# A four-stage decoder on one core: score scale folded into the queries, half tiles, and rotary partners fetched by DMA and combined on GpSimd

## The chip, the cores and the metric

The kernel runs on one core of one Trainium2 chip, in fp32. The time is that of the device, in microseconds (us). The engines are named as the profile names them: PE is TensorE, DVE is VectorE, ACT is ScalarE, POOL is GpSimd, and SP is SyncE, which issues the transfers (DMAs). Each engine works through its own queue in order and waits on semaphores for the others.

## The reference, cut to what matters

The input is 64 sequences of 128 positions and 256 features. Six sublayers are added to it in turn, each on a layer-normalized input. The change lies in the second, fourth and fifth of them, and touches names in the others.

```python
# 1 state-space layer (mamba)
# 2 cross attention, 16 heads of 16, with rotary positions
q = q * cos + rotate_half(q) * sin        # rotate_half: (x1, x2) -> (-x2, x1)
k = k * cos + rotate_half(k) * sin        # x1, x2: the two halves of a head's 16 features
attn_w = softmax(q @ k.T * 16 ** -0.5); out = attn_w @ v @ Wo.T + bo
# 3 gated recurrence: c = sig(f) * c + sig(i) * tanh(g), per step of 128; h = tanh(x Wo + c Uo)
# 4 self attention: 16 query heads, 4 key/value heads, q and k scaled by a factor per position
# 5 cross attention with one head of 256
# 6 mixture of 8 experts, 2 per token, and one shared expert
```

In this kernel the third sublayer steps over the 64 sequences, one step a sequence.

## The kernel before, in words

Sequences are taken in groups of G = 4, so a group has T = 512 columns and there are 16 groups. Activations `X[g]` stay in SBUF for the whole run. There are four stages, each with its own SBUF and PSUM pools. Stage 1 is the state-space layer (0 to 785 us of the profiled execution). Stage 2 is the rotary cross attention together with the recurrence (785 to about 2000). Stage 3 is self attention, the wide cross attention and the routing (about 2000 to 3070). Stage 4 is the experts (3070 to 3482).

In stages 2 and 3 the work is written as Python generators. `run(tasks)` gives each task a turn at which it starts and then advances all active ones by turns, one `yield` at a time. In stage 2 `cross_inputs(g)` starts at turn 16g, the eight `cross_attention(g, b, c)` of a group (four sequences b, two halves c of the heads) at 16g + 16 + 4b + 2c, and `recurrence(g)` at 16g + 42. In stage 3 `self_inputs(g)`, `self_attention(g, b, c)` and `cross_and_route(g)` are placed in the same way. This sets the order in which instructions are handed in; the framework's scheduler then places them, and fixes the order on every engine when the program is built. One group's inputs are thus prepared while the attention of the group before and the recurrence of the one before that are under way.

The parts that matter here:

- `norm` (L166) computes the statistics on DVE, then takes the power −0.5 on POOL (`power`, L163, tile ln_rstd), then writes xn on DVE with four operations, one a sequence (L189). `transposed` (L194) makes pt_ln on PE and copies its two halves to xnT on ACT (L202) and DVE (L204).
- `cross_inputs` (L490): for q and for k two projections into PSUM (proj), of 128 features each, are copied with their bias to raw on ACT (L506). PE multiplies raw by a constant 128x128 permutation with signs (rot, L512). DVE multiplies rot by the sine (L514), POOL multiplies raw by the cosine (L518) and adds both into qT or kT (L519).
- `heads` (L224) is one half-set of eight heads of one sequence. POOL builds a block-diagonal key tile kbd (L284), PE forms the scores s in PSUM (L236), and DVE takes their maximum per row and head (L241) and multiplies it by minus the score scale (L242, tile mx). ACT takes eight exponentials with that bias into e (L245). PE transposes them to pt (L250), ACT and DVE each copy one half to eT (L252, L253), and PE forms av from eT and v (L261).
- v (L532 and stage 3) carries 16 values and 16 ones per head; POOL sets the ones each time with a memset (L533).
- `recurrence` (L565): the input part xg (L572 to L583), then per sequence pu on PE (L593), the sum and tanh in xg, and kept, new and c2 on DVE (L604, L605, L609). Its output xo is stored to DRAM and added to `X[g]` by `self_inputs` in stage 3 (POOL L643, ACT L644, POOL L645).

The PSUM of stages 2 and 3 is divided as `{"mm": 3, "s": 1, "pt": 1, "av": 1}`[...].

Of the kernel before, what the change touches and what calls it, by code (L numbers as in the profile page):

```python
# [15 lines left out]
P = 128  # L16
# [7 lines left out]
C_IDENT, C_UPPER, C_LOWER, C_ROT, C_COS, C_SIN, C_RF, C_ONES = (P * i for i in range(8))  # L24
C_HEAD = 8 * P
# [37 lines left out]
def tile_decoder(ctx: ExitStack, tc: tile.TileContext, a: dict, out: bass.AP):  # L63
# [35 lines left out]
    rot = cst[:, C_ROT:C_ROT + P]  # L99
# [57 lines left out]
    nc.gpsimd.tensor_scalar_mul(fu, fu, 0.5)  # L157

# [35 lines left out]
    def transposed(work, ps, xn, bufs=2):  # L194

        xnT = work.tile([P, 2, T], F32, tag="xnT", name="xnT", bufs=bufs)
        for c in range(2):
            pt = ps.tile([P, T], F32, tag="mm", name="pt_ln")
            for b in range(G):
                nc.tensor.transpose(pt[:, b * P:(b + 1) * P], xn[:, b, c * P:(c + 1) * P], ident)  # L200
            if c == 0:
                nc.scalar.copy(xnT[:, c, :], pt)  # L202
            else:
                nc.vector.tensor_copy(xnT[:, c, :], pt)  # L204
        return xnT

    def project(ps, w, m0, m, rhs):

        o = ps.tile([P, T], F32, tag="mm", name="proj")
        for k in range(2):  # L210
            nc.tensor.matmul(  # L211
                o[:m, :], lhsT=w[:, k, m0:m0 + m], rhs=rhs[:, k, :], start=(k == 0), stop=(k == 1)
            )
        return o

    def project_rows(dst, lhsT, w, b, m=None):

        for k in range(2):
            nc.tensor.matmul(  # L219
                dst, lhsT=lhsT[:, k, b * P:(b + 1) * P], rhs=w[:, k, :] if m is None else w[:, k, m],  # L220
                start=(k == 0), stop=(k == 1),
            )

    def heads(work, ps, b, c, state, q, kbd, v, scale):  # L224
# [9 lines left out]
        for hf in range(2):  # L234
# [4 lines left out]
            )  # L239
        mx = work.tile([P, 8], F32, tag="mx", name="mx", bufs=2)  # L240
        nc.vector.tensor_reduce(mx, s, AX.X, ALU.max)  # L241
        nc.vector.tensor_scalar(mx, mx, -scale, None, ALU.mult)  # L242
        e = work.tile([P, 8, P], F32, tag="e", name="e", bufs=2)
        for h in range(8):
            nc.scalar.activation(e[:, h, :], s[:, h, :], AF.Exp, bias=mx[:, h:h + 1], scale=scale)  # L245
        yield
        yield
        pt = ps.tile([P, 8, P], F32, tag="pt", name="pt")
        for h in range(8):
            nc.tensor.transpose(pt[:, h, :], e[:, h, :], ident)  # L250
        eT = work.tile([P, 8, P], F32, tag="eT", name="eT", bufs=2)
        nc.scalar.copy(eT[:, 0:4, :], pt[:, 0:4, :])  # L252
        nc.vector.tensor_copy(eT[:, 4:8, :], pt[:, 4:8, :])  # L253
# [6 lines left out]
        for vals, which, j, place in vh(c):  # L260
            nc.tensor.matmul(  # L261
                av[j * 32:j * 32 + 32, place, :], lhsT=vals, rhs=eT[:, which, :],
                start=True, stop=True,
            )
        if c == 1:
# [14 lines left out]
            state[b] = o  # L280

# [197 lines left out]
    for c in range(2):  # L479
        for w in (lwq, lwk, lwv):  # L480
            nc.gpsimd.tensor_scalar_mul(w[:, c, :], w[:, c, :], lg[:, c:c + 1])

# [7 lines left out]
    def cross_inputs(g, work, ps, got):  # L490
# [9 lines left out]
        for w, bias, src, tag in ((xwq, xbq, xnT, "qT"), (xwk, xbk, cT, "kT")):  # L500
            t = work.tile([P, 2, T], F32, tag=tag, name=tag, bufs=2)
            raws = []
            for c in range(2):
                pp = project(ps, w, c * P, P, src)
                raw = work.tile([P, T], F32, tag="raw", name="raw", bufs=2)
                nc.scalar.activation(raw, pp, AF.Identity, bias=bias[:, c:c + 1])  # L506
                raws.append(raw)
            yield
            yield
            for c, raw in enumerate(raws):  # L510
                pr = ps.tile([P, T], F32, tag="mm", name="rot")
                nc.tensor.matmul(pr, lhsT=rot, rhs=raw, start=True, stop=True)  # L512
                tv = t[:, c, :].rearrange("p (b t) -> p b t", b=G)
                nc.vector.tensor_tensor(  # L514
                    tv, pr.rearrange("p (b t) -> p b t", b=G), mid(sinT, G), ALU.mult
                )
                rv = raw.rearrange("p (b t) -> p b t", b=G)
                nc.gpsimd.tensor_tensor(out=rv, in0=rv, in1=mid(cosT, G), op=ALU.mult)  # L518
                nc.gpsimd.tensor_tensor(out=tv, in0=tv, in1=rv, op=ALU.add)  # L519
            got[g, tag] = t  # L520
            yield
            yield
        got[g, "c"] = cT

    def cross_attention(g, b, c, work, ps, got):
        tb = slice(b * P, (b + 1) * P)

        def values():
            if c == 0:
                pv = ps.tile([P, T], F32, tag="mm", name="pv")  # L530
                project_rows(pv[:, :D], got[g, "c"], xwv, b)
                v = work.tile([P, 16, 32], F32, tag="v", name="v", bufs=3)  # L532
                nc.gpsimd.memset(v[:, :, 16:32], 1.0)  # L533
# [7 lines left out]
                (v[:, h, :], h % 8, h % 4, h // 4) for h in range(8 * c, 8 * c + 8)  # L541
# [3 lines left out]
            work, ps, b, c, got, got[g, "qT"][:, c, tb],  # L545
            lambda: block_diagonal(work, got[g, "kT"][:, c, tb]), values, 0.25,
# [18 lines left out]
    def recurrence(g, work, ps, got):  # L565
# [6 lines left out]
        xg = work.tile([P, 6, T], F32, tag="xg", name="xg")  # L572
        xo = work.tile([P, G, D], F32, tag="xo", name="xo")
        for part in range(2):
            for c in range(part * 3, part * 3 + 3):
                pp = project(ps, fx, c * P, P, xnT)
                nc.scalar.activation(xg[:, c, :], pp, AF.Identity, bias=fb[:, c:c + 1])
# [7 lines left out]
        for b in range(G):  # L585
            tb = slice(b * P, (b + 1) * P)
            c2 = got["c2"]
            for c0, n in ((0, 4), (4, 2)):
# [8 lines left out]
                pre = xg[:, c0:c0 + n, tb]  # L597
# [6 lines left out]
            nc.vector.scalar_tensor_tensor(kept, xg[:, 0:2, tb], 1.0, c2, ALU.add, ALU.mult)  # L604
            nc.vector.scalar_tensor_tensor(  # L605
                new, xg[:, 2:4, tb], 1.0, xg[:, 4:6, tb], ALU.add, ALU.mult
            )
# [7 lines left out]
    with phase_pool("work2", "left") as work, phase_pool("ps2", space=PSUM) as psp:  # L615
        ps = PsumPool(psp, {"mm": 3, "s": 1, "pt": 1, "av": 1})
        got = {"c2": c2}
# [21 lines left out]
    def self_inputs(g, work, ps, hc, got):  # L639
# [28 lines left out]
        v = work.tile([P, G * 4, 32], F32, tag="v", name="v", bufs=2)  # L668
        nc.gpsimd.memset(v[:, :, 16:32], 1.0)
# [3 lines left out]
    def self_attention(g, b, c, work, ps, got):  # L673
# [3 lines left out]
        def keys():  # L677
            if c == 0:
# [6 lines left out]
                (v[:, b * 4 + j, :], slice(j, 8, 4), j, slice(2 * c, 2 * c + 2)) for j in range(4)  # L685
            ], 1.0 / 16,
# [16 lines left out]
    def wide_attention(g, work, ps):  # L703
        cT = load_ctx(work, g, 1)
# [21 lines left out]
        for b in range(G):  # L726
            tb = slice(b * P, (b + 1) * P)
            for k in range(2):
                nc.tensor.matmul(
                    s[:, b, :], lhsT=qT[:, k, tb], rhs=cT[:, k, tb], start=(k == 0), stop=(k == 1)  # L730
                )
        mx = work.tile([P, G], F32, tag="mx2", name="mx2", bufs=2)
        nc.vector.tensor_reduce(mx, s, AX.X, ALU.max)

        nc.vector.tensor_tensor(mx, mx, qb, ALU.add)
        nc.vector.tensor_tensor(mx, qb, mx, ALU.subtract)
        nc.vector.tensor_scalar(mx, mx, 1.0 / 16, None, ALU.mult)
        e = work.tile([P, G, P], F32, tag="e2", name="e2")
        den = work.tile([P, G], F32, tag="den2", name="den2", bufs=2)
        for b in range(G):  # L740
            nc.scalar.activation(
                e[:, b, :], s[:, b, :], AF.Exp, bias=mx[:, b:b + 1], scale=1.0 / 16,
# [32 lines left out]
    def route(g, work, ps, got):  # L775
# [6 lines left out]
        nc.sync.dma_start(out=XN[g], in_=xnT)  # L782
# [68 lines left out]
    with phase_pool("work3", "left") as work, phase_pool("ps3", space=PSUM) as psp:  # L851
        ps = PsumPool(psp, {"mm": 3, "s": 1, "pt": 1, "av": 1})
# [19 lines left out]
        nc.scalar.copy(yu, pb[:, :D + 1])  # L872
        nc.scalar.copy(ymb, pb[:, D + 1:D + 3])
        for c in range(2):
# [6 lines left out]
            nc.scalar.copy(ym[:, c, :], pw[:, :D])  # L881
# [7 lines left out]
        got = {"full": base}  # L889
# [11 lines left out]
    with phase_pool("work4", "left") as work, phase_pool("ps4", space=PSUM) as psp:  # L901
# [161 lines left out]
        def shared_expert(g):  # L1063
# [5 lines left out]
                gated(project(ps, msg, c * P, P, xnT), project(ps, msu, c * P, P, xnT), f"hs{c}")  # L1069
# [36 lines left out]
def constants():  # L1106
# [10 lines left out]
    for m in range(P):  # L1117
        if d[m] < 8:
            c[m + 8, C_ROT + m] = -1.0
        else:  # L1120
            c[m - 8, C_ROT + m] = 1.0
    inv = (f(1.0) / np.power(f(10000.0), np.arange(0, 16, 2, dtype=f) / f(16))).astype(f)
    ang = i.astype(f)[None, :] * inv[d % 8][:, None]
    c[:, C_COS:C_COS + P] = np.cos(ang.astype(np.float64))
    c[:, C_SIN:C_SIN + P] = np.sin(ang.astype(np.float64))
# [25 lines left out]
def laid_out(v):  # L1151
# [6 lines left out]
    def cat(names, suffix=""):  # L1158
        return np.concatenate([v[f"L0_ffn_{n}"].T for n in names], axis=1)

    b, s, d = v["ctx_1024"].shape
# [8 lines left out]
        "xwq": t("L0_xattn_Wq"), "xbq": v["L0_xattn_bq"], "xwk": t("L0_xattn_Wk"), "xbk": v["L0_xattn_bk"],  # L1170
# [37 lines left out]
```

## Time and profile before

| | us |
|---|---|
| median of 3 runs | 3532.04 (3531.86 to 3532.44) |
| the profiled execution | 3483.77 |
| its span | 3482.0 |
| PE / DVE / ACT / POOL busy | 3176.3 / 2273.2 / 1471.3 / 1302.8 |
| mean granted PE clock | 0.948 |

The span is the time from the first to the last instruction in the trace; the execution has 1.8 us around it. The profiled execution is one run, and was 48 us shorter than the median. Busy times of different engines overlap. Times of places in the trace are counted from the span's start. A half-set of attention occurs 128 times in stage 2 and 128 times in stage 3.

### The profile page before, as it was taken

The numbers are of one execution on the slowest core, as the hardware profiler recorded it, in microseconds if no ns is written. First come the engines' busy times: TensorE is split into PE (matmuls) and PEld (weight loads), VectorE is DVE, ScalarE is ACT, GpSimd is POOL, SyncE is SP. The second block draws the span as 40 slices with busy tenths as digits, with TensorE's granted clock in tenths as the row PEclk, the third lists the DMA queues.
The fourth block names the chain that finished last, engine by engine and source line by source line (L and its number), as shares of the span: only waits on it lengthen the run. The fifth ranks groups of instructions, "written<-read, shape, count | busy, mean of one in ns | idle before, by whom it ended". The sixth has DMA issues, their size and how long they took to land.

```text
span 3482.0 us, 48744 instructions
## 1 busy us (share of the span) xinstructions
PE 3176.3 (91%) x17486; PEld 2033.9 (58%) x17486; DVE 2273.2 (65%) x5498; ACT 1471.3 (42%) x3781; POOL 1302.8 (37%) x1290
## 2 busy tenths in 40 slices
PE   7899999998999999999999767999999999779989
PEld 4555555554666666666666633556566655468845
DVE  7999889965565556655565344777777777543355
ACT  3333333334545555455545234555555555213301
POOL 2444444455332323332332064233333333223276
PEclk9999999999999999999999878999998999789999
DMA  9980000001000000000000011101010101157655
GB/s 312 343 283 1 1 1 1 1 14 30 13 19 13 19 13 13 14 18 19 13 13 7 34 50 41 37 32 42 32 43 32 42 31 43 60 167 227 200 182 180
DMA packets 170658, 229.48 MB, mean 66 GB/s; under 512 B 19504, under 2 KB 142896, under 8 KB 170416
## 3 DMA queue, kind: packets, MB, share of 16 engines
q1 hardware_dynamic: 152448, 180.19, 16.0%
q0 software_dynamic: 17968, 46.18, 4.3%
q8 instruction: 138, 2.26, 0.3%
q14 instruction: 104, 0.85, 0.1%
HBM read 113.71 MB, written 127.93 MB: 69 GB/s over the span
## 4 chain that ended last, share of the span: by engine, by line
PE 62%; DVE 24%; POOL 6%; ACT 4%; DMA 2%; issue 2%; ACTq 0%; DVEq 0%; POOLq 0%; SPq 0%
PE proj L211 17%; PE pt L250 7%; PE s L236 6%; PE pu L593 5%; DVE acc L333 4%; DVE xn L189 4%; PE pgu L1019 4%; PE pv L219 3%; PE pt_ln L200 2%; PE av L261 2%; DVE mx L241 2%; PE pd L1028 2%; PE pxo L219 2%; PE pd L1079 1%; PE po L439 1%
## 5 line engine op out<-in xcount | busy, mean ns | idle before, releaser
L245 ACT ACTIVATE e<-s,mx 128x128 f32<-128x128 f32 x2048 | 555.9, 383 | 479.6 <-DVE mx L242 390.0
L284 POOL TENSOR_TENSOR kbd<-kT,consts 128x512 f32<-128x512 f32 x192 | 202.9, 1057 | 682.3 <-PE s L236 674.0
L253 DVE COPY eT<-pt 128x512 f32<-128x512 f32 x256 | 176.0, 687 | 392.7 <-ACT eT L252 391.7
L250 PE MATMUL pt<-consts,e 128*128 128x128 f32 x2048 | 362.5, 302 | 64.4 <-ACT e L245 62.6
L250 PEld LDWEIGHTS pt<-consts,e 128*128 128x128 f32 x2048 | 258.5, 148 | 180.8 <-ACT e L245 124.5
L211 PE MATMUL proj<-xnT,win 128*128 128x512 f32 x640 | 308.1, 621 | 48.9 <-DVE xc L323 45.0
L241 DVE TENSOR_REDUCE mx<-s 128x8 f32<-128x1024 f32 x256 | 310.5, 1213 | 10.0 <-PE s L236 9.9
L236 PE MATMUL s<-kbd,qT 64*128 64x512 f32 x1024 | 311.1, 686 | 1.5 <-POOL kbd L284 1.5
L252 ACT COPY eT<-pt 128x512 f32<-128x512 f32 x256 | 153.0, 598 | 191.7 <-PE pt L250 190.5
L211 PEld LDWEIGHTS proj<-xnT,win 128*128 128x128 f32 x640 | 119.9, 197 | 192.6 <-issue 112.6
L842 POOL DMA_INDIRECT xs<-xnr,r_rows x128 | 126.6, 989 | 271.5 <-DMA xs<-xnr,r_rows 183.8
L333 DVE SCALAR_TENSOR_TENSOR acc<-proj,convw,acc 128x508 f32<-128x508 f32 (+2 forms) x288 | 209.2, 730 | 7.7 <-ACT acc L329 6.2
L593 PEld LDWEIGHTS pu<-c,fu 128*128 128x128 f32 x1536 | 184.8, 196 | 24.9 <-issue 18.9
L593 PE MATMUL pu<-c,fu 128*128 128x128 f32 x1536 | 187.4, 280 | 8.9 <-DVE c L609 8.9
L392 POOL TENSOR_TENSOR ua<-consts,dt 128x1024 f32<-128x1024 f32 x64 | 121.9, 1906 | 179.7 <-DVE dt L366 150.6
L261 PE MATMUL av<-eT,v 128*32 128x128 f32 (+1 forms) x3072 | 174.5, 328 | 10.0 <-DVE eT L253 9.8
L211 PE MATMUL proj<-xnT,fx 128*128 128x512 f32 x384 | 173.4, 601 | 10.1 <-DVE v L534 9.6
L200 PE MATMUL pt_ln<-consts,xn 128*128 128x128 f32 x640 | 125.6, 316 | 61.5 <-DVE xn L189 39.5
L163 POOL TENSOR_TENSOR ln_rstd<-ln_ve,neghalf 128x4 f32<-128x4 f32 x96 | 98.0, 1021 | 210.4 <-DVE ln_ve L176 158.8
L189 DVE TENSOR_SCALAR xn<-x,ln_mv,ln_rstd 128x256 f32<-128x256 f32 x256 | 142.0, 600 | 40.4 <-POOL ln_rstd L163 40.4
L598 DVE TENSOR_TENSOR xg<-pu,xg 128x512 f32<-128x512 f32 (+1 forms) x128 | 71.4, 558 | 131.6 <-PE pu L593 131.6
L172 DVE BATCH_NORM_STATS2 ln_st<-x 128x6 f32<-128x256 f32 x384 | 146.3, 406 | 13.2 <-DMA x<-in_x_dram 6.2
(266 smaller groups left out, 6508.5 us busy)
## 6 DMA issues: line engine op xcount, KB each, us to landing
xs<-zeros SPq DMA_DIRECT2D x64, 1024.0 KB, 11.1
xs<-xs SPq DMA_DIRECT2D x71, 256.0 KB, 3.4
ys<-y SPq DMA_DIRECT2D x71, 256.0 KB, 2.3
ctxT<-in_ctxT_dram SPq DMA_DIRECT2D x32, 512.0 KB, 3.9
xo<-xo SPq DMA_DIRECT2D x32, 512.0 KB, 3.5
x<-in_x_dram SPq DMA_DIRECT2D x16, 512.0 KB, 8.9
xn<-xnT SPq DMA_DIRECT2D x16, 512.0 KB, 2.6
xnT<-xn SPq DMA_DIRECT2D x16, 512.0 KB, 4.6
```

What stands on the lines that cost most here:

```text
L189: nc.vector.tensor_scalar(xn[:, b, :], x[:, b, :], mv[:, b, 0:1], rstd[:, b:b + 1], ALU.subtract, ALU.mult)
L200: nc.tensor.transpose(pt[:, b * P:(b + 1) * P], xn[:, b, c * P:(c + 1) * P], ident)
L211: nc.tensor.matmul(o[:m, :], lhsT=w[:, k, m0:m0 + m], rhs=rhs[:, k, :], start=(k == 0), stop=(k == 1))
L236: nc.tensor.matmul(s[:, hf * 4:hf * 4 + 4, :], lhsT=q[rows], rhs=kb[rows, :, :], start=True, stop=True,)
L241: nc.vector.tensor_reduce(mx, s, AX.X, ALU.max)
L245: nc.scalar.activation(e[:, h, :], s[:, h, :], AF.Exp, bias=mx[:, h:h + 1], scale=scale)
L250: nc.tensor.transpose(pt[:, h, :], e[:, h, :], ident)
L253: nc.vector.tensor_copy(eT[:, 4:8, :], pt[:, 4:8, :])
L261: nc.tensor.matmul(av[j * 32:j * 32 + 32, place, :], lhsT=vals, rhs=eT[:, which, :], start=True, stop=True,)
L284: nc.gpsimd.tensor_tensor(out=kb, in0=mid(k, 4), in1=last(head, P), op=ALU.mult)
L333: nc.vector.scalar_tensor_tensor(acc[:, :, k:], pv[:, :, :P - k], convw[:, c, 3 - k:4 - k], acc[:, :, k:], ALU.mult, ALU.add,)
L593: nc.tensor.matmul(pu[:, i, :], lhsT=fu[:, k, c * P:(c + 1) * P], rhs=c2[:, k, :], start=(k == 0), stop=(k == 1),)
```

## The change

- The permutation matmul is gone. The columns of the q and k weights and their biases are reordered on the host, so that the two features of a rotary pair lie on neighbouring partitions. ACT writes the projection to `ts[c]` (the tile that becomes qT or kT), two DMAs, one for each parity, copy the odd partitions to the even ones of `others[c]` and the even to the odd, and POOL does all three operations: the cosine in place, the partner times a sine with its sign, and the sum.
- The score scale is multiplied into the query weights once, with a minus sign (xwq and xbq in stage 2, lwq and the combined matrices ym, yu and ymb in stage 3). The scores come out negated and scaled, DVE takes a minimum in place of the maximum, and the multiplication L242 is gone; ACT's exponential uses scale −1.
- xnT, e, eT, pt, xg, and in stage 2 qT and kT, are divided into separate tiles of one half each (xg into four and two parts). The eight exponentials are taken in the order 0, 1, 4, 5, 2, 3, 6, 7, which fills the first half tile first.
- The tiles v are allocated once per stage, three in stage 2 and two in stage 3, and their ones are set once.
- The store of the routed xnT becomes two DMAs.

The diff, cut to its core:

```diff
+    for w in (xwq, xbq):
+        nc.gpsimd.tensor_scalar_mul(w, w, -0.25)
...
-        xnT = work.tile([P, 2, T], F32, tag="xnT", name="xnT", bufs=bufs)
+        xnT = [work.tile([P, T], F32, tag=f"xnT{c}", name=f"xnT{c}", bufs=bufs) for c in range(2)]
...
         mx = work.tile([P, 8], F32, tag="mx", name="mx", bufs=2)
-        nc.vector.tensor_reduce(mx, s, AX.X, ALU.max)
-        nc.vector.tensor_scalar(mx, mx, -scale, None, ALU.mult)
-        e = work.tile([P, 8, P], F32, tag="e", name="e", bufs=2)
-        for h in range(8):
-            nc.scalar.activation(e[:, h, :], s[:, h, :], AF.Exp, bias=mx[:, h:h + 1], scale=scale)
+        nc.vector.tensor_reduce(mx, s, AX.X, ALU.min)
+        e, eT = (
+            [work.tile([P, 4, P], F32, tag=f"{n}{i}", name=f"{n}{i}", bufs=2) for i in range(2)]
+            for n in ("e", "eT")
+        )
+        for h in (0, 1, 4, 5, 2, 3, 6, 7):
+            i, at = tile_of(h)
+            nc.scalar.activation(
+                e[i][:, at, :], s[:, h, :], AF.Exp, bias=mx[:, h:h + 1], scale=-1.0
+            )
...
-        pt = ps.tile([P, 8, P], F32, tag="pt", name="pt")
-        for h in range(8):
-            nc.tensor.transpose(pt[:, h, :], e[:, h, :], ident)
-        eT = work.tile([P, 8, P], F32, tag="eT", name="eT", bufs=2)
-        nc.scalar.copy(eT[:, 0:4, :], pt[:, 0:4, :])
-        nc.vector.tensor_copy(eT[:, 4:8, :], pt[:, 4:8, :])
+        for i in range(2):
+            pt = ps.tile([P, 4, P], F32, tag=f"pt{i}", name=f"pt{i}")
+            for h in range(4):
+                nc.tensor.transpose(pt[:, h, :], e[i][:, h, :], ident)
+            if i == 0:
+                nc.scalar.copy(eT[i], pt)
+            else:
+                nc.vector.tensor_copy(eT[i], pt)
...
+    def values_of(work, n, i):
+        v = work.tile([P, n, 32], F32, tag=f"v{i}", name=f"v{i}")
+        nc.gpsimd.memset(v[:, :, 16:32], 1.0)
+        return v
...
+    nc.gpsimd.tensor_scalar_mul(lwq, lwq, -1.0 / 16)
...
-                raw = work.tile([P, T], F32, tag="raw", name="raw", bufs=2)
-                nc.scalar.activation(raw, pp, AF.Identity, bias=bias[:, c:c + 1])
-                raws.append(raw)
+                nc.scalar.activation(ts[c], pp, AF.Identity, bias=bias[:, c:c + 1])
+
+                nc.sync.dma_start(out=others[c][0:P:2], in_=ts[c][1:P:2])
+                nc.sync.dma_start(out=others[c][1:P:2], in_=ts[c][0:P:2])
             yield
             yield
-            for c, raw in enumerate(raws):
-                pr = ps.tile([P, T], F32, tag="mm", name="rot")
-                nc.tensor.matmul(pr, lhsT=rot, rhs=raw, start=True, stop=True)
-                tv = t[:, c, :].rearrange("p (b t) -> p b t", b=G)
-                nc.vector.tensor_tensor(
-                    tv, pr.rearrange("p (b t) -> p b t", b=G), mid(sinT, G), ALU.mult
-                )
-                rv = raw.rearrange("p (b t) -> p b t", b=G)
-                nc.gpsimd.tensor_tensor(out=rv, in0=rv, in1=mid(cosT, G), op=ALU.mult)
-                nc.gpsimd.tensor_tensor(out=tv, in0=tv, in1=rv, op=ALU.add)
+            for t, other in zip(ts, others):
+                tv, ov = (i.rearrange("p (b t) -> p b t", b=G) for i in (t, other))
+                nc.gpsimd.tensor_tensor(out=tv, in0=tv, in1=mid(cosT, G), op=ALU.mult)
+                nc.gpsimd.tensor_tensor(out=ov, in0=ov, in1=mid(sinT, G), op=ALU.mult)
+                nc.gpsimd.tensor_tensor(out=tv, in0=tv, in1=ov, op=ALU.add)
...
-                v = work.tile([P, 16, 32], F32, tag="v", name="v", bufs=3)
-                nc.gpsimd.memset(v[:, :, 16:32], 1.0)
+                v = got["v"][(g * G + b) % 3]
...
-        xg = work.tile([P, 6, T], F32, tag="xg", name="xg")
+        xgs = [work.tile([P, n, T], F32, tag=f"xg{n}", name=f"xg{n}") for n in (4, 2)]
...
-        ps = PsumPool(psp, {"mm": 3, "s": 1, "pt": 1, "av": 1})
+        ps = PsumPool(psp, {"mm": 3, "s": 1, "pt0": 1, "pt1": 1, "av": 1})
...
-        nc.vector.tensor_tensor(mx, qb, mx, ALU.subtract)
-        nc.vector.tensor_scalar(mx, mx, 1.0 / 16, None, ALU.mult)
+        nc.vector.tensor_tensor(mx, mx, qb, ALU.subtract)
...
-        nc.sync.dma_start(out=XN[g], in_=xnT)
+        for c in range(2):
+            nc.sync.dma_start(out=XN[g][:, c, :], in_=xnT[c])
...
-            nc.scalar.copy(ym[:, c, :], pw[:, :D])
+            nc.scalar.mul(ym[:, c, :], pw[:, :D], -1.0 / 16)
```

`others` has one buffer per half, shared by q and k; `ts` has two.

## Prediction

> **What bounds it now.** I read the page's busy shares and slices first, then the chain, then the waits, then one group of stage 2 singly.
>
> ```profile
> PE 3176.3 (91%) x17486; PEld 2033.9 (58%) x17486; DVE 2273.2 (65%) x5498; ACT 1471.3 (42%) x3781; POOL 1302.8 (37%) x1290
> ...
> PE   7899999998999999999999767999999999779989
> ...
> PEclk9999999999999999999999878999998999789999
> ```
>
> TensorE (PE) is busy 9 tenths or more in most slices. Two dips, near 2000 and 3000 us, are the ends of stage 3.
>
> ```profile
> PE 62%; DVE 24%; POOL 6%; ACT 4%; DMA 2%; issue 2%; ACTq 0%; DVEq 0%; POOLq 0%; SPq 0%
> ```
>
> The chain that ended last is mostly PE, but a quarter is VectorE (DVE): PE is the bound with a slack that DVE and POOL can use up. PE's waits in stage 2 (900 to 1850 us) are short:
>
> ```profile
> PE pt_ln L200 <- DVE kT L514: 19.1, 13, 1.8
> PE proj L211 <- DVE v L534: 9.3, 10, 1.4
> PE pt L250 <- ACT e L245: 8.4, 12, 0.7
> ```
>
> Columns: total, times, longest. One stage-2 group of four sequences, by window:
>
> ```profile
> 1190.00:1263.00 73.00, 69.49 (x457) 45.18 (x456) 43.96 (x93) 37.13 (x102) 24.22 (x24) 1.00 0.06 18
> ```
>
> 73.00 long, PE 69.49, DVE 43.96, ACT 37.13, POOL 24.22, clock 1.00: PE idles 3.5 us a group. Over twelve groups the period is 73.06 us. The same group's end on POOL, in order of time:
>
> ```profile
> 1252.08 1.01 POOL L163 TENSOR_TENSOR ln_rstd<-ln_ve,neghalf 128x4 f32<-128x4 f32 x1 [1.21 <-DVE xn L189]
> 1253.05 2.50 POOL L518 TENSOR_TENSOR raw<-raw,consts 128x512 f32<-128x512 f32 x2
> 1255.50 1.28 POOL L519 TENSOR_TENSOR kT<-kT,raw 128x512 f32<-128x512 f32 x1
> 1256.71 0.32 POOL L533 MEMSET v<- 128x256 f32 x1
> 1256.98 1.27 POOL L519 TENSOR_TENSOR kT<-kT,raw 128x512 f32<-128x512 f32 x1
> 1258.43 1.19 POOL L284 TENSOR_TENSOR kbd<-kT,consts 128x512 f32<-128x512 f32 x1 [0.18 <-PE s L236]
> ```
>
> and on DVE under it:
>
> ```profile
> 1251.54 0.40 DVE L189 TENSOR_SCALAR xn<-x,ln_mv,ln_rstd 128x256 f32<-128x256 f32 x1
> ...
> 1257.23 2.54 DVE L189 TENSOR_SCALAR xn<-x,ln_mv,ln_rstd 128x256 f32<-128x256 f32 x3
> ```
>
> The reader is to see two things. The power for the next normalization (1252.08) runs ahead of k's rotary operations. And one xn takes 0.40 us alone, while three beside POOL's work took 2.54: singly, those that started at 1257.24 and 1258.65 lasted 1.17 and 1.12, ending with kT's sum and with kbd.
>
> **What the Trainium skill says.** "SBUF — State Buffer", section "Who interferes with whom": DVE in its two-port modes, or with two SBUF inputs, and POOL share a port pair under a lock held for a whole instruction. The trace agrees (above). "TensorE: Matmul & The Clock Gate", "What's actually happening": an idle PE falls to half clock, judged in windows of about 3.4 us. Here too: 2498.00 to 2501.40 had PE 2.01 of 3.40, and the two windows after it ran at 0.50. "DMA: Bandwidth & Descriptors", "Anatomy of one DMA": about 2 us fixed cost. The 512 KB store xn<-xnT lands in 2.6 us, so I estimate 2.0 to 2.6 for 128 KB within SBUF.
>
> **Part by part.** Sums are against the profiled execution, 3483.8 us (span 3482.0, and 1.8 around it), which is 48 us or 1.4% under the median 3532.0; I take the same difference from both.
>
> Per stage-2 group:
>
> 1. The rot products go, four a group, each two records. Two of them took 1.82 us start to start (1249.50 to 1251.32), so −3.64 on PE; the row's 66.1 over 16 groups, 4.1, counts overlapping ends.
>
> ```profile
> L512 PE MATMUL rot<-raw,consts 128*128 128x512 f32 x128 | 66.1, 635 | 3.5 <-ACT raw L506 3.5
> L514 DVE TENSOR_TENSOR kT<-rot,consts 128x512 f32<-128x512 f32 x32 | 21.7, 677 | 11.7 <-PE rot L512 11.7
> L518 POOL TENSOR_TENSOR raw<-raw,consts 128x512 f32<-128x512 f32 x64 | 80.2, 1271 | 7.4 <-PE pt L250 4.1 <-PE rot L512 2.0 <-ACT e L245 1.2
> ```
>
> Each row: busy total, mean ns of one, idle before and what ended it. kT's wait for rot goes with them; pt_ln's wait for kT (19.1) was for a PSUM buffer that this product freed. Half clock in about every second group, one window of 3.4 us at half rate, −0.9 (1.7 / 2). The idle 3.5 is taken out to be set anew. PE's need becomes 73.06 − 8.04 = 65.0 us. If nothing else limits it, the whole 8.04 is gained.
>
> 2. DVE loses four rot products (0.68 each) and eight mx scalings (0.33), −5.4 us. Off the path, except that each score's chain to ACT is some 0.2 to 0.3 us shorter.
>
> 3. POOL gains four 128x512 products of 1.27 and loses four memsets of 0.31: +3.8, so 28 of 65 us. Not a bound by sum, but k's six rotary operations become a row of 6 × 1.27 = 7.6 us plus the kbd of 1.04 put among them. In the new order the cross normalization's power stands **behind** that row. Times from k's projection: the recurrence's power ends at 7.3 (as now: 1242.0 to 1249.2), the row at 16.0, the second power at 17.0. Behind the waiting xn stand on DVE the v sum 0.41, three xn of 0.40, the o-to-x sum and the eT copy (0.69): about 3.1, so eT at 20.1. PE would reach the av matmuls that need it at 13.8: 6.3 us of new stall. Of these about 4 show already at pt_ln, since the recurrence's four xn each wait out one POOL operation of the row, 4 × (1.4 − 0.4).
>
> 4. q's row, of the same length, holds off kept, new and c (two SBUF inputs; kept took 1.11 at 1238.99 behind an L519): 0 to 1.3 us more on the recurrence, I take 0.6. Half clock after the longer stall: 0 to 1.7, I take 0.8.
>
> Sum: −8.04 + 6.3 + 0.6 + 0.8 = −0.3; ends −1.6 and +1.5, hence a period of 71.5 to 74.5. Over 14 steady groups −5 (−22 to +21).
>
> 5. The transfers: 128 on SP, eight a group at 0.37 us of issue, 3 us of 73. They wait for ACT's projections; behind them is the ctxT load, needed a group later. k's wait for q's partner tile (one buffer), whose POOL work ended 7 us before k's projection. Landing 2.6 us after ACT's end, at about 7 us, they meet the power's end at 7.3: hidden, at nothing; if landing took 5 us the row would move by 2.4.
>
> 6. Divided tiles: the eT copy on DVE no longer waits for ACT's (391.7 us of DVE idle, mostly unneeded time). Memsets: hidden in POOL's idle, nothing. Set-up scalings on POOL, 1.5 us each: stage 1 +1 (−2 to 2). The first q and k of stage 2 have two POOL operations more each: +3 (0 to 8).
>
> 7. Stage 3, ramp (2000 to 2157): sixteen xo links of about 10.3 us each pace it; in the new order fifteen half-sets of attention lie among them instead of twelve, up to 3 × 7.3 = 22 us of work placed into waiting: I take −12 (−22 to 0).
>
> 8. Stage 3, steady (2165 to 2980): PE waits for e and then pays at half clock.
>
> ```profile
> PE pt L250 <- ACT e L245: 21.7, 16, 1.7
> ...
> ACT e L245 <- DVE r_s L816: 36.3, 12, 3.0
> ```
>
> The wait is small, the half clock behind it is 3.4 to 10.2 us a group, half of it lost: some 2 to 5 us in each of 14 groups. Without the mx scaling and with the routing's second reduction earlier, part goes: −20 (−45 to 0). The sixteen extra stores of xnT are hidden. The recurrence's tail: −2.
>
> Sum: −5 + 1 + 3 − 12 − 20 − 2 = −35, so 3449 for the profiled execution and **3497 us** for the median.
>
> **Rivals.**
>
> - *PE stays the only bound.* If ln_rstd's lateness is covered, for example because the scheduler's other matmuls fill in, stage 2 gains 5.4 to 6 us a group, −80; with steps 6 to 8 −110: 3422. For it: POOL at 37%, and 3.5 us of idle a group show how well the order covers waits. Against: the order on DVE is fixed, and PE's next matmuls wait on it.
> - *POOL's row becomes the bound and costs more than the matmuls.* Place: the k row, with the power and the DVE queue behind it. Each of its six operations, lengthened by DVE operations that hold the port pair (kbd 1.19 instead of 1.04), and DVE held in turn, give 12 us of stall instead of 7.7: period 77.3, +60, and less the −30 elsewhere **3562**. It decides from about 10 us of stall a group, where the stage loses the 32 us that the others bring. For it: 2.54 for three xn. Against: ACT and PE work on scores needs no shared ports.
> - *The change moves work and nothing more*: the recurrence (pu, tanh, kept, c2) sets the period. It would leave 73 us whatever goes from PE, and 3500; against it, its waits are only 8.9 us at L593 in all. It lies within the forecast.
>
> **Numbers.** A measurement here tells about 0.2%, 7 us, from no change. Forecast (stage 2 about unchanged, 3475 to 3530) 0.50; first rival 0.27; second 0.23. Of the forecast 0.40 is faster, 0.09 within 7 us, 0.01 slower; of the second rival 0.02 is within. Faster 0.67, same 0.11, slower 0.22. The range 3425 to 3550 takes in most of the first rival and the near half of the second.
>
> **What would show it.** No rot rows, POOL about 60 us busier, no wait of eT for ACT's copy. Right: new PE waits at pt_ln for xn and at av for eT in stage 2 of some 4 and 2 us a group, xn's mean above 600 ns, the power behind k's row, a period of 71.5 to 74.5. A period of 65 to 68 shows the first rival, above 75 the second. Transfers to the partner tiles landing later than 5 us, or kbd waiting for them, would make step 5 wrong; half-clock windows in stage 3 as long as now, step 8.

## The result, and the profile after

| | before | after |
|---|---|---|
| median, us | 3531.95 (3530.02 to 3532.44, 4 runs) | 3511.76 (3507.84 to 3521.81, 4 runs) |
| ratio | | 0.9948, 95% interval 0.9926 to 0.997 |
| the profiled execution's span, us | 3482.0 | 3519.9 |

The change gains about half a per cent. The two profiled spans say the opposite, and only because of the last stage, which the change hardly touches. From the first expert matmul (pgu) to the end of the span, the trace of before has 393 us and that of after 446; in twelve later traces, one of the changed kernel among them, it is 392 to 396. Up to the first pgu the changed kernel is 16 us ahead in this profile and 21 in the later one. The medians above are some 47 us longer than those of the same two kernels on later chips (3485 and 3464), close to the 53 us by which the last stage of this profile is longer. So the long last stage seems to belong to these executions and not to the change, but no trace of before was taken in one of them.

The page of after, for busy shares and the chain that ended last:

```profile
PE 3170.8 (90%) x17358; PEld 2039.9 (58%) x17358; DVE 2237.2 (64%) x5162; ACT 1469.6 (42%) x3781; POOL 1372.8 (39%) x1282
...
PE 60%; DVE 21%; POOL 7%; issue 5%; ACT 3%; DMA 3%; another core or an unknown queue 1%; SPq 0%; POOLq 0%; DVEq 0%; ACTq 0%
```

POOL is 70 us busier and DVE 36 less. PE is still the bulk of the chain. One stage-2 group (columns as in the prediction: length, then busy PE, PEld, DVE, ACT, POOL, then clock), and PE's waits in stage 2, 900 to 1850 us:

```profile
1037.00:1109.00 72.00, 68.71 (x451) 45.25 (x449) 41.61 (x82) 37.47 (x102) 28.07 (x24) 0.98 0.09 30
```

```profile
PE pt_ln L201 <- DVE xn L190: 24.9, 26, 1.0
PE av L274 <- DVE eT L266: 16.5, 15, 3.5
PE pu L614 <- DVE c L629: 4.3, 13, 0.6
```

The wait for kT is gone, and three new waits stand in its place: for xn, for eT behind it, and for the recurrence's c. The end of the same group on POOL, in order of time (k's projection began at 1088.57):

```profile
1095.05 1.02 POOL L164 TENSOR_TENSOR ln_rstd<-ln_ve,neghalf 128x4 f32<-128x4 f32 x1 [6.24 <-DVE ln_ve L177]
1096.04 1.27 POOL L537 TENSOR_TENSOR kT<-kT,consts 128x512 f32<-128x512 f32 x1
...
1102.44 1.04 POOL L307 TENSOR_TENSOR kbd<-kT,consts 128x512 f32<-128x512 f32 x1
1103.43 1.26 POOL L539 TENSOR_TENSOR kT<-kT,other 128x512 f32<-128x512 f32 x1
1104.66 1.01 POOL L164 TENSOR_TENSOR ln_rstd<-ln_ve,neghalf 128x4 f32<-128x4 f32 x1
```

and on DVE:

```profile
1097.98 3.37 DVE L190 TENSOR_SCALAR xn<-x,ln_mv,ln_rstd 128x256 f32<-128x256 f32 x3
...
1105.71 0.41 DVE L190 TENSOR_SCALAR xn<-x,ln_mv,ln_rstd 128x256 f32<-128x256 f32 x1 [2.64 <-POOL ln_rstd L164]
```

The row of six rotary operations, with one kbd among them, fills POOL from 1096.04 to 1104.69. The second power starts only then, at 16.1 us after k's projection (the same to 0.1 us in eleven of twelve groups, 17.3 in the other); in the trace of before it started at 10.1, ahead of the row. Beside the row, three xn take 3.37 us; after it, one takes 0.41.

Where the time went, between starts of the same matmuls, in the traces of before and of the changed kernel repeated on another chip (called after_again below), whose last stages are alike:

| stretch | before | after_again | difference |
|---|---|---|---|
| start to the first xwk projection | 798.0 | 797.4 | −0.6 |
| to the first fx projection (stage 2 filling) | 99.0 | 97.1 | −1.9 |
| twelve stage-2 periods | 12 × 73.06 | 12 × 72.21 | −10.2 |
| to the first lwk projection (rest of stage 2) | 246.9 | 242.4 | −4.4 |
| to the fourth lwk projection (ramp of stage 3) | 175.1 | 162.8 | −12.3 |
| twelve stage-3 periods | 12 × 58.02 | 12 × 58.86 | +10.1 |
| to the first pgu | 197.2 | 195.0 | −2.2 |
| pgu to the end of the span | 392.8 | 394.4 | +1.6 |

A period is the time from one group's start to the next: in stage 2 between fx projections (the input part of the recurrence), in stage 3 between lwk projections (self attention). The ramp is the stretch before stage 3 reaches its steady period; it runs to the fourth lwk projection, which some expectations below count as the third after the first. Half clock is time at a granted PE clock of 0.50; half of it is counted as lost.

### The profile page after: what moved, and what is told of

The parts are those of the page before. It is cut to its first block, busy times and chain, and to the rows that moved or that the text cites. A ratio compares the mean times of both kernels' runs of the same rounds, so it can differ in the third digit from the quotient of the medians.

```text
span 3519.9 us, 48443 instructions
## 1 busy us (share of the span) xinstructions
PE 3170.8 (90%) x17358; PEld 2039.9 (58%) x17358; DVE 2237.2 (64%) x5162; ACT 1469.6 (42%) x3781; POOL 1372.8 (39%) x1282
## 4 chain that ended last, share of the span: by engine, by line
PE 60%; DVE 21%; POOL 7%; issue 5%; ACT 3%; DMA 3%; another core or an unknown queue 1%; SPq 0%; POOLq 0%; DVEq 0%; ACTq 0%
PE proj L215 16%; PE pt L262 7%; PE s L240 6%; PE pu L614 5%; PE pv L223 4%; DVE acc L356 3%; DVE xn L190 3%; PE av L274 3%; PE pt_ln L201 3%; PE pgu L1041 2%; PE pr L718 2%; PE pxo L223 2%; PE pd L1104 2%; DVE m L438 1%; DVE y L449 1%
## 5 line engine op out<-in xcount | busy, mean ns | idle before, releaser
L190 DVE TENSOR_SCALAR xn<-x,ln_mv,ln_rstd 128x256 f32<-128x256 f32 x256 | 169.0, 705 | 76.8 <-POOL ln_rstd L164 76.8
L614 PEld LDWEIGHTS pu<-c,fu 128*128 128x128 f32 x1536 | 181.7, 194 | 32.9 <-issue 16.1
L274 PE MATMUL av<-eT,v 128*32 128x128 f32 (+1 forms) x3072 | 181.9, 324 | 20.6 <-DVE eT L266 20.1
L1065 POOL DMA_INDIRECT ys<-ys,t_yrow x128 | 124.6, 974 | 95.0 <-DVE x L1077 45.7
L452 POOL TENSOR_TENSOR y<-y,zs 128x512 f32<-128x512 f32 x64 | 81.7, 1276 | 191.6 <-DVE y L449 185.3
```

The source lines that it names most:

```text
L190: nc.vector.tensor_scalar(xn[:, b, :], x[:, b, :], mv[:, b, 0:1], rstd[:, b:b + 1], ALU.subtract, ALU.mult)
L274: nc.tensor.matmul(av[j * 32:j * 32 + 32, place, :], lhsT=vals, rhs=eT[i][:, at, :], start=True, stop=True,)
L614: nc.tensor.matmul(pu[:, i, :], lhsT=fu[:, k, c * P:(c + 1) * P], rhs=c2[:, k, :], start=(k == 0), stop=(k == 1),)
```

## The experiments

They ran on other chips, where before takes 3485 to 3486 us; each is compared with runs of before on its own chip. The totals expected of the first four were written for the level of the first chip, 3532; they are read as ratios. The theory: PE saves the rot matmuls, and POOL's row in front of the normalization gives the time back. The rivals: the row is hidden and something else sets the period, or the swap is the gain and the rest of the change costs.

### The change repeated, and the partner rows by matmul again

after_again has no edit.

> The changed kernel itself, beside the variants that follow, on one chip. Theory: about 3512 us, 0.994 to 0.996 of before, stage-2 period 72.5 us, stage-3 period 58.9 with some 9.7 us of half clock a group. The last stage (from the first expert's weights to the end) took 407 us in the profile of before and 461 in that of after, though the change touches nothing in it; if that is a matter of the execution and not of the kernel, it is other than 461 here, between 400 and 460. Rival: the change makes the last stage slower; then again about 461.

Measured: 3463.83, 0.9939 (0.9919 to 0.9958); stage-2 period 72.21, stage-3 period 58.86, half clock 9.7 us a stage-3 group; last stage 394.4. So the theory held: the 446 of the first profile did not come again.

pe_rot:

```diff
-nc.sync.dma_start(out=others[c][0:P:2], in_=ts[c][1:P:2])   # and the other parity
+pr = ps.tile(...); nc.tensor.matmul(pr, lhsT=rot, rhs=raw, start=True, stop=True)
-nc.gpsimd.tensor_tensor(out=ov, in0=ov, in1=mid(sinT, G), op=ALU.mult)
+nc.vector.tensor_tensor(tv, pr, mid(sinT, G), ALU.mult)
```

> The changed kernel with the partner rows made by a permutation matmul on PE again, the sine product on DVE and four rotary operations a q or k pair on POOL, as before; scale folding, divided tiles and prepared v stay. Theory: the swap of matmul for DMA and POOL is about even (PE saves 3.6 us a group and pays back 3.1), so stage 2 has a period of 72.5 to 73.1 here, no pt_ln wait for xn of 25 us but again the wait for kT; stage 3 is that of the changed kernel (ramp 13 us shorter than before, period 58.9); total within 10 us of after, 3510 to 3522. Rival A: the scale and the divided tiles made the gain of stage 2 and the DMAs cost time; then the period falls below 72 and the total to 3495 to 3505. Rival B: the DMA rotary brings the gain and the rest costs; then the total is 3530 or more.

Measured: 3461.04, 0.9928 (0.9911 to 0.9945), which is 3507 at the level of the first chip, between the two ranges; period 71.72, no half clock in stage 2. The period is rival A's: without the swap the kernel is as fast, and stage 2 is 0.5 us a group shorter. The theory's "even" holds for the total, but the gain of stage 2 comes from the rest. The wait for kT, which the theory expected back, did not come.

### One part at a time

scale_only, on the kernel before:

```diff
+for w in (xwq, xbq): nc.gpsimd.tensor_scalar_mul(w, w, -0.25)      # lwq, ym, yu, ymb by -1/16
-nc.vector.tensor_reduce(mx, s, AX.X, ALU.max)
-nc.vector.tensor_scalar(mx, mx, -scale, None, ALU.mult)
+nc.vector.tensor_reduce(mx, s, AX.X, ALU.min)
```

> The kernel before with nothing but the score scale folded into the query weights (and minimum for maximum); tiles undivided, rotation by matmul, v set each time. Theory A (the shorter chain from scores to exponentials is what the rest of the change brings): stage-2 period 71.7 to 72.4, the ramp of stage 3 (first to third self-attention projection) 160 to 166 us instead of 175, stage-3 period 58.5 to 59, total 3460 to 3472. Theory B (the divided tiles bring it): period 72.8 to 73.1, ramp 172 to 177, stage-3 period 57.8 to 58.3, total 3480 to 3488 as before.

Measured: 3456.92, 0.9919 (0.9902 to 0.9935); period 71.71, ramp 161.9, stage-3 period 58.40. Theory A, with a total 3 us under its range and a stage-3 period just short of 58.5: the scale alone brings as much as the whole change. Its PE waits, 900 to 1740 us:

```profile
PE pt L251 <- ACT e L246: 14.4, 11, 1.3
PE proj L213 <- DVE v L536: 6.7, 11, 0.6
```

The wait of pt_ln for kT, 19.1 us in before, is gone although the rot matmuls and the product L514 are still there. The same place of a group in before, on DVE and on ACT:

```profile
1251.86 1.21 DVE L241 TENSOR_REDUCE mx<-s 128x8 f32<-128x1024 f32 x1
1252.99 0.68 DVE L514 TENSOR_TENSOR kT<-rot,consts 128x512 f32<-128x512 f32 x1
1253.59 0.76 DVE L242 TENSOR_SCALAR mx<-mx 128x8 f32<-128x8 f32 x1
```

```profile
1254.44 2.17 ACT L245 ACTIVATE e<-s,mx 128x128 f32<-128x128 f32 x8 [2.33 <-DVE mx L242]
```

and in scale_only:

```profile
1247.85 1.21 DVE L243 TENSOR_REDUCE mx<-s 128x8 f32<-128x1024 f32 x1
```

```profile
1249.16 2.17 ACT L246 ACTIVATE e<-s,mx 128x128 f32<-128x128 f32 x8 [3.98 <-DVE mx L243]
```

In before the exponentials start 1.37 us after the reduction: a product of kT stands between, and the multiplication L242 takes 0.76 us beside POOL's work, where its mean is 0.33. In scale_only they start 0.10 us after it. The product of kT comes at the same time in both (11.0 us after k's projection), so it is not what became faster. What changed is that PE now takes pt before pt_ln: it waits once, 1.31 us for e, where it had waited 1.45 for kT and 0.71 for e. The half clock in stage 2, 1.7 us a group, is gone too. Whether the earlier e or the new order on PE counts for more was not separated. In the ramp (2000 to 2165) PE is busy 126.9 us instead of 107.3: more attention stands among the xo links (the additions of the recurrence's output, which pace the ramp).

tiles_only: pe_rot with the scale multiplication put back.

```diff
-nc.vector.tensor_reduce(mx, s, AX.X, ALU.min)
+nc.vector.tensor_reduce(mx, s, AX.X, ALU.max)
+nc.vector.tensor_scalar(mx, mx, -scale, None, ALU.mult)
```

> The kernel before with nothing but the divided tiles, the order of the exponentials, and the prepared v (rotation by matmul, scale multiplication L242 kept). Theory (PE never waits for the eT copies, so dividing them is worth nothing): period 72.8 to 73.3, stage-3 period 57.9 to 58.9, total within 7 us of before, 3478 to 3492. Rival (the divided tiles bring part of the gain): period under 72.5, total under 3472.

Measured: 3481.26, 0.9984 (0.9977 to 0.9991); period 72.43, ramp 174.5, stage-3 period 57.99. The period meets the rival's number, the total the theory's: a small gain, 5 us. pe_rot differs from it in the scale alone: the exponentials at the place above start 1.4 us after the reduction here and 0.1 there, and the total is 20 us lower there.

dma_only, on the kernel before:

```diff
-nc.tensor.matmul(pr, lhsT=rot, rhs=raw, start=True, stop=True)
+nc.sync.dma_start(out=others[c][0:P:2], in_=t[1:P:2, c, :])        # and the other parity
-nc.vector.tensor_tensor(tv, pr, mid(sinT, G), ALU.mult)
+nc.gpsimd.tensor_tensor(out=ov, in0=ov, in1=mid(sinT, G), op=ALU.mult)
```

> The kernel before with nothing but the rotation changed: partner rows by transfers within SBUF, six POOL operations for q and for k, no permutation matmul; tiles undivided, scale multiplication L242 and memsets as before. Theory (the swap alone is even or a loss, since PE's 3.6 us come back as stall behind the row): stage-2 period 72.6 to 74.2, ramp about 175 us, total 3480 to 3500. Rival (the swap is what made the changed kernel faster): period 71.8 to 72.4, total 3460 to 3472.

Measured: 3512.23, 1.0078 (1.0061 to 1.0095); period 75.15, 0.95 above the upper end given, with 5.7 us of half clock a group. The swap alone is a loss of 26 us. PE's waits, 900 to 1740 us:

```profile
PE av L261 <- DVE eT L253: 44.8, 16, 5.3
...
```

In one group of it a multiplication of mx took 1.46 us beside the row, ahead of the normalization's xnT, and the eT copy stood on DVE behind three xn of 1.35 to 1.42 us, where in the changed kernel it stands behind one. This suggests why the swap costs more here; it was not tried singly. The three parts alone sum to −28, −5 and +26, so −7, where the whole change has −22 on its chip. So the parts are not additive: the swap costs 26 us alone and about 3 beside the other two (pe_rot against after_again, within their intervals).

### The row: longer, absent, or elsewhere

row_plus:

```diff
+if tag == "kT":
+    nc.gpsimd.tensor_tensor(out=spare, in0=ov, in1=mid(cosT, G), op=ALU.mult)
```

> The changed kernel with one more POOL product of 128x512 (1.27 us) at the end of k's rotary row, into a tile that nobody reads, ahead of the second power. Theory (the end of the row, through the power and the eT copy behind it on DVE, sets when PE goes on): the period of stage 2 rises from 72.2 by 1.3 to 2.1 us, the av waits for eT grow by about 1.3 us a group, total 18 to 30 us above the changed kernel on this chip (3464), so 3482 to 3494. Rival (the row is hidden and PE's own work sets the period): 72.0 to 72.5, total 3460 to 3469.

Measured: 3479.89, 0.9987 (0.998 to 0.9994), 16 us above after_again, which ran on another chip; period 73.55, so +1.34 for one operation of 1.27. The total is 2 us under the range given.

```profile
PE pt_ln L201 <- DVE xn L190: 21.7, 23, 1.0
PE av L274 <- DVE eT L266: 21.6, 19, 3.5
...
```

The second power and the end of the eT copy are both 1.2 us later than in after_again (17.3 and 21.0 us after k's projection instead of 16.1 and 19.8). The wait for eT grew from 12.5 us to 21.6, about 0.8 a group where 1.3 was expected; half clock is 4.8 us a group instead of 3.1, and half of that difference makes up the rest. The end of the row decides.

no_rotary:

```diff
-nc.sync.dma_start(...)                                             # all partner transfers
-nc.gpsimd.tensor_tensor(...)                                       # all rotary operations
```

> The changed kernel with the whole rotary step left out: no partner transfers, no products, no sums, so q and k go unrotated into the scores. It shows what stage 2 takes when neither PE nor POOL pays for rotation. Theory (PE is the bound once POOL's row is gone): period 66 to 68.5, no pt_ln wait for xn and hardly an av wait, total 55 to 85 us under the changed kernel: 3380 to 3410. Rival (another chain, the recurrence's, sets about 72 us whatever goes): period 70.5 to 72.

Measured: 3383.45, 0.9705 (0.9689 to 0.9722); period 66.80, no PE wait of stage 2 in the view, no half clock. One group:

```profile
1150.00:1217.00 67.00, 66.98 (x450) 44.04 (x449) 36.68 (x84) 37.82 (x105) 12.66 (x11) 1.00 0.05 17
```

PE is busy 66.98 of 67.00: this is its own need. So no other chain holds stage 2 at 72, and the changed kernel pays 5.4 us a group for the rotary step.

xn_1port keeps xn out of the two-port mode: the Trainium skill's "SBUF — State Buffer", section "Who interferes with whom", excepts the form of tensor_scalar that also writes out its accumulator. The form also changes what xn holds, so the run tells of the order and the ports alone:

```diff
 nc.vector.tensor_scalar(xn[:, b, :], x[:, b, :], mv[:, b, 0:1], rstd[:, b:b + 1],
-    ALU.subtract, ALU.mult)
+    ALU.subtract, ALU.mult, accum_out=spare[:, b:b + 1])
```

> The changed kernel, with the DVE operation that writes xn (L190) also summing into a small tile that nobody reads, which by the Trainium skill keeps it out of the two-port mode; the order on POOL and DVE is the same. Theory (port pair locked by POOL's row): one xn takes 0.4 to 0.45 us also beside POOL operations, its mean falls from 705 ns to under 460, the pt_ln waits for xn in stage 2 fall from 25 us to under 10, period 70 to 71.7, total 3480 to 3500. Rival (the row delays by its order alone, the power behind it): xn's mean falls or not, period 72.3 to 72.7, total within 7 us of after, 3505 to 3519.

Measured: 3477.37, 0.998 (0.997 to 0.9989), period 74.95. xn by groups, and PE's waits, 900 to 1750 us:

```profile
L191 DVE TENSOR_SCALAR_CACHE_REDUCE xn<-x,ln_mv,ln_rstd 128x256 f32<-128x256 f32 x256 | 126.4, 535 | 109.3 <-POOL ln_rstd L164 109.3
```

```profile
PE av L276 <- DVE eT L268: 50.6, 22, 5.5
...
```

Period and total lie above both ranges, though each side had one thing right. The lock is real: with one port in use every xn takes 0.53 to 0.54 us, beside the row too, and the pt_ln waits are all but gone. But the time did not come back. The xnT copy was 3 us earlier, DVE then idled 5.21 us for the second power instead of 2.25, and PE waited at av for what it had not waited for at pt_ln, and longer. PE idles 5.2 us a group instead of 3.6, with 6.2 us of half clock instead of 3.1; the idle and half of the clock make 3.0, about the 2.7 that the period grew. The eT copy is only 0.4 us later (20.2 instead of 19.8), so why PE idles that much more was not located. Freeing xn of the lock moves the wait; it does not remove it while the power stands behind the row.

early_pow:

```diff
+mv, rstd = early(work, g)          # bn_stats, bn_aggr, power
+for _ in range(8 if g else 0): yield
-xn = norm(work, g)
+xn[:, b, :] = (X[g][:, b, :] - mv) * rstd                           # as before, on DVE
```

> The changed kernel, with the statistics and the power of the cross normalization computed eight turns earlier, so that the power stands ahead of k's rotary row on POOL; xn is still written where it was. Theory: the av waits for eT in stage 2 (16.5 us) go, and with them part of the half clock behind them: period 70.5 to 71.8, total 3485 to 3502. Rival (the row and the lock on xn decide, and the power is hidden): av waits shrink but pt_ln's grow by as much, period 72.2 to 72.8, total within 7 us of after.

Measured: 3458.58, 0.9925 (0.9908 to 0.9942); period 71.62, so −0.6, and a total that the intervals do not tell from after_again's. The waits for eT hardly fell (10.7 us) and those for xn stayed (23.6). With the power out of the way, the eT copy is only 1 us earlier, because the recurrence's xn are still held by the row and everything behind them on DVE with them. The period is in the theory's range, the total (0.9925 of 3532 is 3506) at the rival's edge. With xn_1port this suggests that both effects of the row, the power behind it and the lock beside it, have to go.

minus_early adds to it:

```diff
+if c and tag == "kT":
+    nc.vector.tensor_tensor(turn, ts[c], mid(cosT, G), ALU.mult)     # in place of POOL's product
```

> The changed kernel with the cross normalization's power eight turns earlier (as early_pow), and one of k's two cosine products on DVE, into a tile of its own, right after ACT's copy: k's row on POOL has five operations, DVE one more of some 0.7 us. Theory: xn and eT behind the row come 1 to 1.3 us earlier than in early_pow; stage-2 period 70.2 to 71.0, total 3443 to 3453. Rival (the lock merely moves to the new DVE product, or another wait is as late): 71.4 to 71.9, total 3455 to 3462.

Measured: 3493.68, 1.0025 (1.0015 to 1.0036), period 74.24. Missed altogether. The order had shifted: one cosine product now stands ahead of the first power too, xn starts 9.6 us after k's projection instead of 7.5, and all PE waits are at pt_ln (52.5 us). In this order one operation in front of a power cost more than one taken out behind it saved.

row_late; it also starts the next group's `cross_inputs` five turns earlier:

```diff
+added = nc.gpsimd.tensor_tensor(out=X[g], in0=X[g], in1=mid(xbo, G), op=ALU.add)
...
+with tc.issue_after(got["added", g + 1]):        # order on POOL only, no wait
     ...                                          # k's six rotary operations
```

> The changed kernel with k's rotary row queued on POOL behind the next group's cross normalization (both powers, then the addition of the output bias, then the six rotary operations); the cross normalization is handed in five turns earlier, the row four turns later. Same operations, same transfers, same sums. Theory (the row in front of the normalizations is what PE waits for): xn's mean falls to about 540 ns, the pt_ln and av waits of stage 2 go, the period comes near the 66.8 us of the kernel without rotation: 66.8 to 69; the total is 45 to 75 us under the changed kernel, 3389 to 3419. Rival (the row delays something wherever it stands: then kbd waits for kT and the scores for kbd): a new PE wait of s for kbd, period 70 to 73, total 3440 to 3475.

Measured: **3404.67, 0.9763 (0.9747 to 0.9779)**, 82 us under before; period 67.78. POOL in one group, in order of time:

```profile
1151.58 1.02 POOL L165 TENSOR_TENSOR ln_rstd<-ln_ve,neghalf 128x4 f32<-128x4 f32 x1 [6.24 <-DVE ln_ve L178]
1153.12 1.04 POOL L308 TENSOR_TENSOR kbd<-kT,consts 128x512 f32<-128x512 f32 x1 [0.53 <-PE s L241]
1155.10 1.01 POOL L165 TENSOR_TENSOR ln_rstd<-ln_ve,neghalf 128x4 f32<-128x4 f32 x1 [0.94 <-DVE xn L191]
1158.06 2.35 POOL L522 TENSOR_TENSOR x<-x,xbo 128x1024 f32<-128x1024 f32 x1 [1.95 <-DVE xn L191]
1160.37 1.27 POOL L546 TENSOR_TENSOR kT<-kT,consts 128x512 f32<-128x512 f32 x1
```

and the DVE between them, with the waits of PE, 900 to 1740 us:

```profile
1153.56 1.40 DVE L191 TENSOR_SCALAR xn<-x,ln_mv,ln_rstd 128x256 f32<-128x256 f32 x3
...
1156.61 1.36 DVE L191 TENSOR_SCALAR xn<-x,ln_mv,ln_rstd 128x256 f32<-128x256 f32 x4
```

```profile
PE pu L624 <- DVE c L639: 3.5, 11, 0.4
PE pa L286 <- ACT kT L533: 1.0, 1, 1.0
```

The same operations, in another order: four xn take 1.36 us, the second power starts 10.0 us after k's projection instead of 16.1, and kbd waits for no kT that PE would notice. This is 1.0 us from the kernel without rotation, and it beats both kernels. Starting `cross_inputs` five turns earlier was not run without the move of the row. early_pow, which started only the statistics and the power earlier, gained 0.6 us a group.

scale_late is scale_only with the rotation of dma_only and the same late row.

> The kernel before with the folded scale and the rotation by transfers, k's row queued late as in row_late; tiles undivided, v set each time. Theory (scale and the moved rotation are what counts, the divided tiles are worth nothing): stage-2 period as in row_late, within 0.5 us, total within 8 us of row_late. Rival (the late row needs the divided tiles, since the eT copy on DVE waits for ACT's): period over 1 us longer than in row_late.

Measured: 3416.56, 0.9797 (0.9781 to 0.9814), period 68.64, 0.86 above row_late, with 15.8 us of waits of av for eT that row_late does not have. The theory's limits (half a microsecond, 8 us) are passed, the rival's microsecond is not reached. Beside the late row, the divided tiles and the prepared v are worth 12 us together.

## Why the prediction was right or wrong, point by point

The range and the side were right. The forecast's median was 15 us too low on that chip; as a ratio it had 0.990 where 0.9948 and 0.9939 were measured. That it came so near is in part luck: stage 3's steady part was 30 us worse than forecast, and stage 2, with its filling and its end, about 12 us better.

1. *Stage 2, steps 1 to 4.* Right in mechanism: the power ends up behind k's row, and the new waits are those for xn and eT. The sum was right too (a period of 71.5 to 74.5 was given, 72.5 and 72.2 came), but by luck, since its terms were off both ways. The power begins at 16.1 (16.0 was given), the eT copy ends at 19.8 (20.1). PE's need is 66.8 by no_rotary, not 65.0: of 8.04 us, 6.3 came off. Part of the excess lies in the rot matmuls, since PE is busy 69.8 us a period in pe_rot and 66.8 in no_rotary, 3.0 for rot and not 3.64. Against that, the stalls in the trace are 24.9, 16.5 and 4.3 us over some 13 groups: 1.9 at pt_ln, 1.3 at av and 0.3 at pu, where about 4, 2 and 0.6 were given. So 3.5 a group and not 6.9, with 2.0 for half clock and not 0.8; 66.8 + 3.5 + 2.0 is 72.3.
2. *What gains in stage 2, step 2.* Wrong. The prediction gave the mx scaling next to nothing there ("Off the path, except that each score's chain to ACT is some 0.2 to 0.3 us shorter"). scale_only shows 1.35 us a group. Where PE waits, that chain became 1.3 us shorter and not 0.3, because the multiplication stood behind a product of kT on DVE and was itself slow beside POOL.
3. *The transfers, step 5.* Right: hidden. The page of after_again gives the landing, the last number of the line:

```profile
other<-qT SPq DMA_DIRECT2D x64, 128.0 KB, 2.0
```

   That is the low end of the estimate of 2.0 to 2.6, and kT's transfers land in 2.0 as well. POOL waited for q's in its own idle time, and for k's 1.0 us in the whole run.

4. *Divided tiles, step 6.* The wait of DVE for ACT's copy is gone, and worth 5 us with the prepared v in tiles_only; beside the late row, 12. Stage 2's filling was to cost 3 and gained 1.9.
5. *The ramp, step 7.* Right: −12 was given, −12.3 came, and scale_only has it in full; dma_only and tiles_only (174 us) do not.
6. *Stage 3's steady part, step 8.* Wrong: −20 was given, +10 came. PE's waits in it, 2165 to 2870 us:

```profile
PE pt L262 <- ACT e L254: 25.5, 24, 1.5
```

   There are two waits for e a group now. The second, 0.8 to 1.5 us, stands where before waited 0.4 us for r_sel, and the first became shorter (1.1 instead of 1.4 us in single groups), so PE idles 2.1 us a group in both. Half clock is what grew: 9.7 us a group instead of 8.0, and half of the difference is the 0.85 that a period lost. The prediction expected it to shrink with the wait. Kernels with the scale multiplication kept have 8.0 to 8.5 and periods of 58.0 to 58.1; scale_only has 8.5 as well, with 58.40, so the scale alone does not explain all of it. Why the order puts the second wait there was not tried.
7. *The rivals.* PE as the only bound was 0.27, at 3422, and its stage 2 is what row_late nearly reaches (67.78), not the change. The row as a bound that costs more than the matmuls is dma_only, at 75.15 and not the 77.3 given. With the prediction's own terms, 73.06 − 8.04 + 12, that figure should have been 77.0. The change lies between the two, because the scale came with it.

## What to carry to other kernels

Before moving work off the busiest engine, look for something short and urgent that will queue behind it on the engine that takes it; busy shares do not show that. Here moving the long row helped far more than moving the short operation in front of it. Where a change has several parts, run each alone: here the smallest edit carried the gain, and the largest gave its own away until it was put in another place. When removing one wait makes another grow by as much, as in xn_1port, look further back in the chain.

## What the runs showed of the hardware that was not expected

- The lock works on both sides: beside each other, POOL's operations of 1.27 us became 1.31 to 1.46, and xn's 0.41 became 1.35 to 1.42. The Trainium skill's "SBUF — State Buffer", section "Who interferes with whom", says that the one that issues second blocks for the other's whole instruction, and that a DVE form with one SBUF input outside the two-port modes does not contend. xn_1port agrees: its xn, at 0.54, was never held.
- Half clock does not follow the total stall alone. minus_early idles 5.2 us a group and has 7.1 us of half clock; dma_only idles 5.7 and has 5.7. In stage 3, before and after both idle 2.1 us and have 8.0 and 9.7.
- A transfer of every second partition took SP 0.47 and 0.60 us to issue, against 0.37 for ctxT, a transfer four times as large.
